# Rational filter and convolution: filter taps by butterflies, and a shifted input copied inside SBUF

## The chip, the cores and the metric

The kernel runs on one core of one Trainium2 chip. The metric is the device time of one execution in microseconds. Three runs of the kernel before took 27,779.66, 27,808.01 and 27,824.27 us; the median is 27,808.01.

## The reference

The input `x` is (4, 512, 512, 16), float32. Layer 0 convolves it over the two image axes with a filter whose transform is a quotient of two short polynomials, then layer 1 applies a 3x3 normalised convolution. Both add their result to their input. Cut to what matters here:

```python
def _L0_conv_ref(x, h0, numerators, denumerator):
    a = jnp.pad(denumerator, ((0, 0), (0, 0), (1, 0), (1, 0)), constant_values=1.0)
    b = jnp.pad(numerators, ((0, 0), (0, 0), (0, 0), (1, 0), (1, 0)), constant_values=0.0)
    H_truncated = jnp.fft.rfft2(b, s=(l1, l2)) / jnp.fft.rfft2(a, s=(l1, l2))
    h_truncated = jnp.fft.irfft2(H_truncated, s=(l1, l2))
    H = jnp.fft.rfft2(h_truncated, s=(2 * l1, 2 * l2))
    H_full = h0 + H[0]
    X = jnp.fft.rfft2(x, s=(2 * l1, 2 * l2), axes=(-3, -2))
    Y = jnp.einsum('...hwi,ijhw->...hwj', X, H_full)
    y = jnp.fft.irfft2(Y, s=(2 * l1, 2 * l2), axes=(-3, -2))
    return y[..., :l1, :l2, :]

x = x + _L0_conv_ref(_gn(x), L0_conv_h0, L0_conv_numerators, L0_conv_denumerator)
x = x + _L1_conv_ref(_gn(x), L1_conv_kernel, L1_conv_bias, L1_conv_radius)
```

`_gn` is a group norm over 8 groups of channels. There are 16 input channels i and 16 output channels j, so 256 filters.

## The kernel before, in words

The Fourier transforms are matmuls with constant matrices, all in float32. A float32 matmul shows as two instructions in the trace. The kernel has five stages, one after the other.

**The filter phase** (`filter_phase`, lines 223 to 430) makes the filter's spectrum `g_d` in DRAM. It loops over the output channel j, over two halves h of the even frequencies of the second axis, and over the input channel i: 16 x 2 x 16 = 512 spectra. For each, `spectrum` evaluates both polynomials by matmuls over 18 rows (`pab`, line 320), copies them out of PSUM on ScalarE (`ab`), and divides: VectorE makes the reciprocal and the products `m` and `sp`, GpSimd makes `dn`, `x` and the sums in `m` (lines 330 to 344). `taps` multiplies `sp` by the constant `dinv` (`pg`, line 353) and ScalarE copies the result into a staging tile `st`. Before the change, `dinv` takes the spectrum over the first axis's frequency k1 straight to the form that the product stage wants: even frequencies of blocks of 8 taps. The calls are staggered by one: `spectrum` of the next i is issued ahead of `taps` of the one before. After all i of a (j, h), `st` is stored to `g_d` (line 405). `odd` loads four blocks of `g_d`, makes the odd frequencies of the second axis (`pt`, line 381, 16 matmuls of 128x512) and stores them. One `odd` call follows every second spectrum, beginning with the second j. The group norm's statistics of `x` are gathered beside the first spectra.

**The forward phase** transforms `x` over the second axis into `x_d`. **The product phase** (`conv_phase`, lines 578 to 763) takes 513 rows of frequencies one at a time, as a pipeline written out in `step(n)`. A row's filter tile is `g`, its input tile `x`. `x_part` transforms four batches of the input over blocks (`px`, line 643) into `xf`. On its last batch GpSimd stores `xf` to a DRAM buffer `xf_d` (line 648). `load_xe` (line 658), issued by SyncE (SP) one step ahead, reads it back as `xe`: eight copies, each shifted by one block of 16 partitions. `g_part` transforms the filter (`pg`, line 675), using the upper and lower 64 partitions as two matmuls of 64x128 with the constant `dg`, into `gh`. `mix` multiplies the two (`pm`, line 691, 32 columns of the array each). `over_q` and `over_g` are the inverse over blocks (`pz`, line 708, and `py`, line 724), and GpSimd stores the result to `y_d`. `evict` copies PSUM to SBUF on VectorE and ScalarE in turn (lines 608 and 610).

**The inverse phase** transforms back over the second axis and **the layer 1 phase** does the rest.

The tile framework places the waits and orders each engine's instructions ahead of time with a scheduler of its own, roughly by the order in the program[...]. SP issues the loads, GpSimd (POOL) the stores of `xf` and of the product.

Of the kernel before, what the change touches and what calls it, by code (L numbers as in the profile page):

```python
# [29 lines left out]
F32 = mybir.dt.float32  # L36
# [15 lines left out]
XF = F * 2 * B  # L52
# [8 lines left out]
def constants():  # L61
# [3 lines left out]

    r = np.array([[v for u in range(8) for v in ((8 * q + u, -(8 * q + u) % S) if q + u else (0, 32))]
                  for q in range(4)])
    k1 = (64 * np.arange(8)[None, :, None] + r[:, None, :]).reshape(-1)
    p9 = np.arange(9)
    ang = 2 * np.pi * np.outer(p9, k1) / N  # L70
    c["e1"] = np.concatenate([np.cos(ang), -np.sin(ang)], 0)
    e2 = np.zeros((4, 32, 2, 2, P))
    a2 = (2 * np.pi * np.outer(p9, np.arange(256)) / N).reshape(9, 2, P)
# [4 lines left out]
    t = np.arange(N)  # L78
    back = np.exp(2j * np.pi * np.outer(k1, t) / N) / N
    over_s = np.exp(-2j * np.pi * np.outer(np.arange(S) - 31.5, 2 * np.arange(33)) / F)  # L80
    d = np.zeros((4, P, 2, 4, 4, 8, 8))
    for cc in range(2):
        taps = (back * (1, 1j)[cc]).reshape(N, S, 8)
        for plane in range(2):
            v = np.einsum("kse,sr->kre", (taps.real, taps.imag)[plane], over_s)
            re, im = v.real[:, :32], np.concatenate([v.imag[:, 32:], v.imag[:, 1:32]], 1)
            for part, w_ in (((0, re), (2, im)), ((3, re), (1, im)))[plane]:
                d[:, :, cc, part] = w_.reshape(4, P, 4, 8, 8)
    c["dinv"] = np.stack([d[q, :, :, :, q] for q in range(4)], 1).reshape(P, -1)

    f_all = 2 * np.pi * np.outer(np.arange(S) - 31.5, np.arange(F)) / F
    dg = np.zeros((4, 32, F))
    for r in range(33):
        full = np.zeros((2, S), complex)
        full[0, r] += 1.0
        full[0, -r % S] += -1.0 if r else 0.0
        full[1, r] += 1j
        full[1, -r % S] += 1j if r < 32 else 0.0
        for part in range(2):
            if r == 32 * (1 - part):  # L100
                continue
            sig = (np.exp(2j * np.pi * np.outer(np.arange(S) - 31.5, 2 * np.arange(S)) / F) @ full[part]) / S
            assert abs(sig.imag).max() < 1e-12
            if part == 0:
                dg[0, r] = dg[3, r] = sig.real @ np.cos(f_all)
            else:
                v = -(sig.real @ np.sin(f_all))
                dg[2, r % 32], dg[1, r % 32] = v, -v
    c["dg"] = dg.reshape(P, F)
# [33 lines left out]
    for q in range(4):  # L143
        for cg in range(2):
            for s0 in range(4):
                co, si = turn(np.array(cg + q * (s0 - 31.5)), 4)
                for j in range(C):
                    q1[q, cg, j, s0, 0, j], q1[q, cg, j, s0, 1, j] = co, si
# [4 lines left out]
    for s0 in range(4):  # L153
        for cx in range(2):
            for c2 in range(2):
                n = gg[:, None] * (s0 - 31.5) + 4 * gg[:, None] * s1[None, :] + 32 * (cx + c2)
                co, si = turn(n, F)
                for b2 in range(2):
                    ig[:, cx, b2, s0, c2, 0, b2, :] = co / F
                    ig[:, cx, b2, s0, c2, 1, b2, :] = si / F  # L160
# [59 lines left out]
def filter_phase(tc, cst, h0, num, den, g_d, beside):  # L220
    nc = tc.nc
    with ExitStack() as ctx:
# [4 lines left out]
        hp = ctx.enter_context(tc.tile_pool(name="f_h", bufs=2))  # L227
        stp = ctx.enter_context(tc.tile_pool(name="f_stage", bufs=3))
# [9 lines left out]
        dinv = load_const(nc, cp, cst, "dinv").rearrange("p (k c n) -> p k c n", k=4, c=2)  # L238
# [108 lines left out]
        def taps(sp, st, i):  # L347

            for kp in range(2):
                pg = ps_g.tile([P, 2, 2, 2 * 64], F32, name="pg")  # L350
                for k in range(2):
                    for c in range(2):
                        nc.tensor.matmul(  # L353
                            pg[:, k].rearrange("p a x -> p (a x)"), sp[:, 2 * kp + k, c, :],
                            dinv[:, 2 * kp + k, c, :], start=(c == 0), stop=(c == 1),
                        )
                for a in range(2):
                    nc.scalar.copy(
                        st[a][:, :, i].rearrange("p (q k x) -> p k q x", q=2, k=4)[:, 2 * kp : 2 * kp + 2],
                        pg[:, :, a].rearrange("p k (q x) -> p k q x", q=2),  # L360
                    )

        def odd(j, tb):

            first = ((0, 96), (64, 32))[tb // 8]
            at = [((first[c] + 4 * (tb % 8)) * C + j) * 8 * C for c in range(2)]
            step = [C * 8 * C, 4], [1, 8 * C]
            ev = evp.tile([P, 2, 2, 32 * C], F32, name="ev_in")
            for h in range(2):
                for c in range(2):  # L370
                    nc.sync.dma_start(
                        out=ev[:, h, c].rearrange("p (s e) -> p s e", s=4),
                        in_=dram(g_d[h], None, at[c], *step),
                    )
            for hh in range(2):
# [13 lines left out]
                for c in range(2):  # L389
                    nc.sync.dma_start(  # L390
                        out=dram(g_d[2 + hh], None, at[c], *step),
# [6 lines left out]
        def finish(j, h, i, sp):  # L398
            nonlocal st
            if i == 0:  # L400
                st = [stp.tile([P, N, C], F32, name=f"st{a}", tag="st") for a in range(2)]
            taps(sp, st, i)
            if i == C - 1:
                for a in range(2):
                    nc.sync.dma_start(
                        out=dram(g_d[h], None, a * G_ROW // 2 + j * 8 * C,
                                 [C * 8 * C, 64], [1, 8 * C]),
                        in_=st[a].rearrange("p (r e) i -> p r (e i)", e=8),
# [634 lines left out]
```

## Time and profile before

| | |
|---|---|
| median of three runs | 27,808.01 us |
| profiled execution, its own time | 27,779.66 us |
| profiled execution, span of the core | 27,777.9 us |
| granted TensorE clock, mean | 0.905 |
| busy: TensorE (PE), VectorE (DVE), ScalarE (ACT), GpSimd (POOL) | 92%, 42%, 28%, 24% |
| steady filter, per spectrum (2000 to 8000 us) | 17.05 us |
| product phase, per step | 21.34 us |

Busy shares are averages over stages that have different limits, so each stage is read on its own. The 40 digits of a slice row are tenths of busy time in slices of 694 us: the filter covers about the first 13, the forward phase up to the 16th, the product phase the 16 after that. A group line gives busy time, mean duration of one instruction, and the idle time of the engine before it with what ended it. "PEld" is the load of weights into TensorE, which runs beside matmuls. In a line of the order in time the first number is the start in us, the second the length, and a bracket names an idle time and its releaser.

### The profile page before, as it was taken

To read this page: it belongs to the slowest core of one execution; us is meant where nothing else is said; L and a number is where in the kernel's file an instruction comes from. 1 tells how busy PE (TensorE), PEld (TensorE's weight loads), DVE (VectorE), ACT (ScalarE), POOL (GpSimd) and SP (SyncE) were. 2 spreads that over 40 slices of the span, in tenths; PEclk is the share of its full clock that TensorE was granted. 3 is DMA by queue.
4 is the path that set the end of the run, shared out by engine and by line. 5 is a ranking of instruction groups with operands and counts; after the bars stand their busy time and mean duration, and the time that the engine had idled before them with its cause. 6 is when DMAs were issued, how large, how long until landed. Compare 5 with 4: busy or idle time off the path is not lost. (4 is left out here: it accounts for less than half of the span.)

```text
span 27777.9 us, 539638 instructions
## 1 busy us (share of the span) xinstructions
PE 25559.6 (92%) x240412; PEld 16342.2 (59%) x240412; DVE 11700.4 (42%) x16077; ACT 7865.0 (28%) x13480; POOL 6775.9 (24%) x8210
## 2 busy tenths in 40 slices
PE   9999999999999999999999999999999999566666
PEld 6556666666665445666666666666666544455556
DVE  6555444544443112333333333333333200577777
ACT  4333333333332111222222222222222100122222
POOL 5444444444442000000000000000000000355555
PEclk8888888888888999999999999999999999766666
DMA  3433333333334334888888888888888633211110
GB/s 97 137 93 98 87 97 88 98 86 100 85 98 129 102 107 150 323 319 321 321 319 323 318 321 318 321 322 320 321 323 322 236 111 111 79 53 54 49 43 21
DMA packets 2987106, 5014.77 MB, mean 181 GB/s; under 512 B 97482, under 2 KB 2064932, under 8 KB 2885958
## 3 DMA queue, kind: packets, MB, share of 16 engines
q1 hardware_dynamic: 2725894, 4105.78, 43.0%
q0 software_dynamic: 203584, 740.22, 6.8%
q10 hardware_dynamic: 55296, 134.24, 1.7%
q8 instruction: 1883, 30.85, 0.4%
q14 instruction: 449, 3.68, 0.0%
HBM read 3502.38 MB, written 1477.44 MB: 179 GB/s over the span
## 5 line engine op out<-in xcount | busy, mean ns | idle before, releaser
L381 PE MATMUL pt<-ev_in,c_todd 128*128 128x512 f32 x8192 | 3683.0, 608 | 52.0 <-DMA ev_in<-g_d 33.8
L353 PE MATMUL pg<-c_dinv,sp 128*128 128x256 f32 x8192 | 2665.3, 492 | 102.5 <-DVE sp L344 91.9
L381 PEld LDWEIGHTS pt<-ev_in,c_todd 128*128 128x128 f32 x8192 | 1589.2, 195 | 1977.5 <-issue 1879.5
L675 PEld LDWEIGHTS pg<-c_dg,g 64*128 64x128 f32 x32832 | 2040.3, 189 | 1061.2 <-issue 965.2
L675 PE MATMUL pg<-c_dg,g 64*128 64x128 f32 x32832 | 2461.8, 287 | 139.2 <-issue 138.5
L353 PEld LDWEIGHTS pg<-c_dinv,sp 128*128 128x128 f32 x8192 | 2012.2, 253 | 855.0 <-issue 327.9
L691 PEld LDWEIGHTS pm<-xe,gh 128*32 128x32 f32 x131328 | 1899.9, 110 | 1043.8 <-issue 1037.5
L708 PE MATMUL pz<-c_iq,yf 128*128 128x128 f32 x16416 | 2419.8, 291 | 73.2 <-issue 63.6
L945 PE MATMUL pc<-l_band,xn 128*128 128x160 f32 (+3 forms) x9024 | 1824.3, 370 | 714.4 <-DVE e_y L968 713.5
L333 DVE RECIPROCAL dn<-dn 128x256 f32<-128x256 f32 x1024 | 1786.7, 1745 | 1637.8 <-POOL dn L332 1637.7
L648 POOL DMA_DIRECT2D xf_d<-xf x513 | 365.9, 713 | 8524.6 <-ACT xf L610 4284.9
L608 DVE COPY gh<-pg 128x512 f32<-128x512 f32 x2052 | 1419.5, 692 | 2060.7 <-PE pg L675 2060.7
L320 PE MATMUL pab<-c_e,u 18*128 18x256 f32 x8192 | 2223.3, 428 | 54.0 <-ACT ab L325 53.9
L724 PE MATMUL py<-z,c_ig 128*64 128x256 f32 x8208 | 2242.4, 705 | 2.1 <-ACT z L610 1.4
L691 PE MATMUL pm<-xe,gh 128*32 128x64 f32 x131328 | 2084.7, 220 | 168.8 <-issue 164.6
L708 PEld LDWEIGHTS pz<-c_iq,yf 128*128 128x128 f32 x16416 | 2016.6, 193 | 331.5 <-issue 77.6
L643 PE MATMUL px<-c_dfs,x 128*128 128x512 f32 x4104 | 2136.1, 602 | 29.2 <-issue 16.5
L945 PEld LDWEIGHTS pc<-l_band,xn 128*128 128x128 f32 x9024 | 1556.0, 240 | 973.5 <-DVE e_y L968 740.0
L320 PEld LDWEIGHTS pab<-c_e,u 18*128 18x128 f32 x8192 | 1641.3, 207 | 631.5 <-issue 262.4
L610 ACT COPY gh<-pg 128x512 f32<-128x512 f32 x2052 | 1201.2, 585 | 2189.3 <-PE pg L675 2189.3
L556 PE MATMUL pf<-xw,c_fwd 128*128 128x512 f32 x4096 | 1781.5, 593 | 3.7 <-DVE xw L547 3.7
L792 PE MATMUL po<-c_inv,yt 128*128 128x512 f32 x4096 | 1760.3, 593 | 14.2 <-DMA yt<-y_d 14.2
(149 smaller groups left out, 27208.7 us busy)
## 6 DMA issues: line engine op xcount, KB each, us to landing
xe<-xf_d SPq DMA_DIRECT2D x513, 4096.0 KB, 14.2
xf_d<-xf POOLq DMA_DIRECT2D x513, 1024.0 KB, 6.4
g<-g_d SPq DMA_DIRECT2D x511, 1024.0 KB, 5.5
g_d<-st SPq DMA_DIRECT2D x64, 4096.0 KB, 31.4
ev_in<-g_d SPq DMA_DIRECT2D x1024, 256.0 KB, 4.8
g_d<-ot SPq DMA_DIRECT2D x1024, 256.0 KB, 2.3
xt<-in_x SPq DMA_DIRECT2D x128, 1024.0 KB, 9.7
x_d<-xo SPq DMA_DIRECT2D x128, 1024.0 KB, 5.1
```

The source lines that it names most:

```text
L320: nc.tensor.matmul(pp[:, k].rearrange("p c n -> p (c n)"), us[n][q, k1 : k1 + P], e2[q, h, :], start=True, stop=True,)
L333: nc.vector.reciprocal(dn, dn)
L353: nc.tensor.matmul(pg[:, k].rearrange("p a x -> p (a x)"), sp[:, 2 * kp + k, c, :], dinv[:, 2 * kp + k, c, :], start=(c == 0), stop=(c == 1),)
L381: nc.tensor.matmul(pt, todd[:, kc, m : m + P], ev[:, kc % 2, kc // 2], start=(kc == 0), stop=(kc == 3),)
L556: nc.tensor.matmul(pf.rearrange("p i s t -> p (i s t)"), fwd[:, w, col : col + P], xw[:, w, 4 * i4 : 4 * i4 + 4, :].rearrange("p i h -> p ...
L643: nc.tensor.matmul(px.rearrange("p l f c -> p (l f c)"), t[:, b], dfs.rearrange("p l n -> p (l n)"), start=True, stop=True)
L675: nc.tensor.matmul(pg[c][:, k], g[half, 4 * j4 + k], dg[half], start=True, stop=True)
L691: nc.tensor.matmul(pm[32 * q : 32 * q + 32, gi], gh[:, f].rearrange("p c j -> p (c j)"), xe[:, :, f, :], start=True, stop=True,)
L708: nc.tensor.matmul(pz[:, t], y[:, at].rearrange("p g x -> p (g x)"), iq, start=True, stop=True)
L724: nc.tensor.matmul(py[64 * half : 64 * half + 64, odd], ig[:, s0, c2], z[:, :, :, 2 * s0 + c2, :].rearrange("p t h j -> p h j t"), start=( ...
L792: nc.tensor.matmul(po, yt[kc][:, m // 4, odd, bh, :], inv[:, kc, :], start=(kc == 0), stop=(kc == 7),)
L945: nc.tensor.matmul(pc[:, lo:hi, :].rearrange("p w j -> p (w j)"), blocks[q][0][:, h * P + dh : h * P + dh + P], bands[dh][:, o : o + hi - ...
```

## The change

The filter's `dinv` no longer includes the transform over blocks. `taps` first combines the four quarters of k1 (a radix-4 butterfly: `s` and `w` of the even outputs on GpSimd, `d` and `w` of the odd ones on VectorE), then multiplies each of the four results by a 128-point transform; `st` holds taps in their natural order. `g_part` then does the whole transform of a block with the constant `dfs` that `x_part` uses, over all 128 partitions, in eight calls of two matmuls in place of four calls of eight; `dg` is gone. `x_part` stores nothing: `load_xe` copies `xf` to `xe` inside SBUF by 15 transfers issued on SP. `over_g` reads `z` with the 16 output channels innermost in place of the 8 block positions, and its eviction puts them in the old order. The `pg` pool of the product phase has two banks in place of three, the `pz` pool two in place of one. The constants `iq` and `ig` lose a shift of 31.5 blocks.

```diff
         def taps(sp, st, i):
-            for kp in range(2):
-                pg = ps_g.tile([P, 2, 2, 2 * 64], F32, name="pg")
-                for k in range(2):
+            s = bt.tile([P, 2, 2, P], F32, name="s")
+            d = bt.tile([P, 2, 2, P], F32, name="d")
...
+            nc.gpsimd.tensor_add(fl(s), fl(sp[:, 0:2]), fl(sp[:, 2:4]))
+            nc.vector.tensor_sub(fl(d), fl(sp[:, 0:2]), fl(sp[:, 2:4]))
+            w = hp.tile([P, 4, 2, P], F32, name="w")
+            nc.gpsimd.tensor_add(w[:, 0], s[:, 0], s[:, 1])
+            nc.gpsimd.tensor_sub(w[:, 2], s[:, 0], s[:, 1])
+            nc.vector.tensor_sub(w[:, 1, 0], d[:, 0, 0], d[:, 1, 1])
+            nc.vector.tensor_add(w[:, 1, 1], d[:, 0, 1], d[:, 1, 0])
+            nc.vector.tensor_add(w[:, 3, 0], d[:, 0, 0], d[:, 1, 1])
+            nc.vector.tensor_sub(w[:, 3, 1], d[:, 0, 1], d[:, 1, 0])
+            for rp in range(2):
+                pg = ps_g.tile([P, 2, 2, P], F32, name="pg")
+                for r2 in range(2):
+                    r = 2 * rp + r2
                     for c in range(2):
                         nc.tensor.matmul(
-                            pg[:, k].rearrange("p a x -> p (a x)"), sp[:, 2 * kp + k, c, :],
-                            dinv[:, 2 * kp + k, c, :], start=(c == 0), stop=(c == 1),
+                            pg[:, r2].rearrange("p c t -> p (c t)"), w[:, r, c, :],
+                            dinv[:, r, (1 - c) * P : (3 - c) * P],
+                            start=(c == 0), stop=(c == 1),
                         )
-                for a in range(2):
+                for c in range(2):
                     nc.scalar.copy(
-                        st[a][:, :, i].rearrange("p (q k x) -> p k q x", q=2, k=4)[:, 2 * kp : 2 * kp + 2],
-                        pg[:, :, a].rearrange("p k (q x) -> p k q x", q=2),
+                        st[c][:, :, i].rearrange("p (t r) -> p r t", r=4)[:, 2 * rp : 2 * rp + 2, :],
+                        pg[:, :, c, :],
                     )
...
-        ps_g = ctx.enter_context(tc.tile_pool(name="h_psg", bufs=3, space=PSUM))
+        ps_g = ctx.enter_context(tc.tile_pool(name="h_psg", bufs=2, space=PSUM))
...
-        ps_z = ctx.enter_context(tc.tile_pool(name="h_psz", bufs=1, space=PSUM))
+        ps_z = ctx.enter_context(tc.tile_pool(name="h_psz", bufs=2, space=PSUM))
...
             if b == B - 1:
-                dst = xf_d[n % 4]
-                nc.gpsimd.dma_start(
-                    out=bass.AP(tensor=dst.tensor, offset=dst.offset,
-                                ap=[[XF, P], [P * XF, 2], [1, XF]]),
-                    in_=state.pop(("xf", n)).rearrange("p l f h c k -> p l (f h c k)"),
-                )
                 del state["x", n]
         def load_xe(n):
             xe = xep.tile([P, 8, F, 2 * B], F32, name="xe")
-            src = xf_d[n % 4]
-            nc.sync.dma_start(
-                out=xe.rearrange("p t f x -> p t (f x)"),
-                in_=bass.AP(tensor=src.tensor, offset=src.offset,
-                            ap=[[XF, P], [C * XF, 8], [1, XF]]),
-            )
+            xf = state.pop(("xf", n)).rearrange("p l f h c k -> p l (f h c k)")
+            for k in range(8):
+                m = P - C * k
+                nc.sync.dma_start(out=xe[:m, k].rearrange("p f x -> p (f x)"), in_=xf[C * k :, 0])
+                if k:
+                    nc.sync.dma_start(out=xe[m:, k].rearrange("p f x -> p (f x)"), in_=xf[: C * k, 1])
...
-            pg = [ps_g.tile([P, 4, F], F32, name=f"pg{c}", tag="pg") for c in range(2)]
-            for k in range(4):
-                for c in range(2):
-                    half = slice(64 * c, 64 * c + 64)
-                    nc.tensor.matmul(pg[c][:, k], g[half, 4 * j4 + k], dg[half], start=True, stop=True)
-            for c in range(2):
-                evict(gh[:, :, c, 4 * j4 : 4 * j4 + 4], pg[c].rearrange("p j f -> p f j"))
+            pg = ps_g.tile([P, 2, F * 2], F32, name="pg")
+            for k in range(2):
+                nc.tensor.matmul(pg[:, k], g[:, 2 * j2 + k], dfs[:, 0], start=True, stop=True)
+            evict(gh.rearrange("p f c j -> p j (f c)")[:, 2 * j2 : 2 * j2 + 2], pg)
...
-            py = ps_y.tile([P, 2, 2, C, 8], F32, name="py")
+            py = ps_y.tile([P, 2, 2, 8, C], F32, name="py")
...
-                            z[:, :, :, 2 * s0 + c2, :].rearrange("p t h j -> p h j t"),
+                            z[:, :, :, 2 * s0 + c2, :].rearrange("p t h j -> p h t j"),
...
-            evict(yo, py.rearrange("p o h j t -> p (o h j t)"))
+            evict(yo.rearrange("p (x j t) -> p x j t", x=4, j=C), py.rearrange("p o h t j -> p (o h) j t"))
...
                 if after:
-                    g_part(n + 1, k)
+                    g_part(n + 1, 2 * k)
                 if soon:
                     over_q(n - 1, k)
                 if late:
                     x_part(n + 2, k)
+                if after:
+                    g_part(n + 1, 2 * k + 1)
```

## The prediction

> **What bounds the kernel now.** I read the page first (busy shares, slices, groups by cost), then busy time by stage, then the order in time inside the two stages that the change touches: the filter phase (0 to 8720 us, where the last `g_d<-st` store is issued) and the spectral product `conv_phase` (about 10,950 to 21,900 us).
>
> ```profile
> span 27777.9 us, 539638 instructions
> PE   9999999999999999999999999999999999566666
> DVE  6555444544443112333333333333333200577777
> PEclk8888888888888999999999999999999999766666
> ```
>
> TensorE is busy nine tenths or more of both stages, but in the first 13 slices, the filter, its clock is only 0.8. Why shows in 3 us windows of the filter (columns: length, then busy PE, PEld, DVE, ACT, POOL, then granted clock, DMA share, GB/s):
>
> ```profile
> 5074.00:5077.00 3.00, 3.00 (x8) 2.07 (x7) 3.00 (x4) 0.83 (x2) 2.06 (x4) 0.50 0.00 0
> 5086.00:5089.00 3.00, 3.00 (x9) 1.33 (x8) 0.00 (x0) 0.58 (x1) 0.00 (x0) 1.00 0.17 50
> ```
>
> There are two kinds of stretch. In one VectorE never rests and TensorE does `pab` and `pg` at half clock; in the other TensorE runs the odd-frequency matmuls `pt` at full clock while VectorE and GpSimd rest. The order in time gives the cycle:
>
> ```profile
> 5048.69 12.18 PE L381 MATMUL pt<-ev_in,c_todd 128*128 128x512 f32 x28
> 5060.80 3.72 PE L320 MATMUL pab<-c_e,u 18*128 18x256 f32 x16
> 5064.44 5.41 PE L353 MATMUL pg<-c_dinv,sp 128*128 128x256 f32 x16
> 5069.78 4.78 PE L320 MATMUL pab<-c_e,u 18*128 18x256 f32 x16
> ```
> ```profile
> 5072.53 0.93 DVE L342 TENSOR_TENSOR sp<-m,dn 128x256 f32<-128x256 f32 x1 [0.62 <-POOL m L340]
> 5073.49 0.58 DVE L344 COPY sp<-z 128x8 f32<-128x8 f32 x1
> ```
>
> Two spectra and one odd block take about 34 us (window 2000 to 8000: 22 pairs of stores, so 352 spectra, 17.05 us each). The second spectrum's `sp` is done at 5074.07 and its `pg` starts at 5074.49: **no margin** between the elementwise chain and TensorE there. The chain of the spectrum after it runs under the `pt` burst.
>
> In `conv_phase` a step of 21.34 us repeats 513 times, and TensorE's work fills it:
>
> ```profile
> 15011.20 4.29 PE L724 MATMUL py<-z,c_ig 128*64 128x256 f32 x16
> 15015.42 2.00 PE L691 MATMUL pm<-xe,gh 128*32 128x64 f32 x128
> 15017.35 1.16 PE L675 MATMUL pg<-c_dg,g 64*128 64x128 f32 x16
> 15018.44 1.16 PE L708 MATMUL pz<-c_iq,yf 128*128 128x128 f32 x8
> 15019.44 1.02 PE L643 MATMUL px<-c_dfs,x 128*128 128x512 f32 x2
> ```
>
> From start to start: 4.22, 1.93 (twice a step), 1.09, 1.00 and 0.95 (four times each), 20.2 us in all. The DMA engines are 85% busy. `xe` is issued 15017.96 and takes 14.2 us, so lands at 15032.2; the next step's `mix` starts at 15036.77: 4.6 us of slack.
>
> ```profile
> xe<-xf_d SPq DMA_DIRECT2D x373, 4096.0 KB, 14.2
> q1 hardware_dynamic: 496141, 2057.01, 69.0%
> ```
>
> [...] `sp` takes 349 ns at least and 985 at most, the longest when it starts beside a GpSimd operation of some 720.
>
> ```profile
> L342 DVE TENSOR_TENSOR sp<-m,dn x2048: 349/426/985, 41.5 to 8703.3; 128x256 f32<-128x256 f32 x187
> L339 POOL TENSOR_TENSOR m<-m x1024: 712/724/1108, 36.1 to 8701.5; 128x256 f32<-128x256 f32 x171
> ```
>
> [...] `py` reads its moving side at a step of 1 KB and takes 705 ns; other matmuls of 256 columns take 380 in the median (`pg`, line 353).[...] 16 of the half-height `pg` start over 1.09 us, 68 ns each, though one takes 272; 16 `py` over 4.22 us, 264 each, though one takes 705.[...]
>
> **The change, part by part.** Sums are made against the profiled execution (27,779.66 us, span 27,777.9), the fastest of the three runs; the median lies 28 us above, which I add at the end.
>
> *Filter, matmuls.* `taps` keeps 8 matmuls of 128x256 and 4 ScalarE copies of 256 elements per spectrum; the copies write at a step of 256 B in place of 64 B. ScalarE is 37% busy here (741 of 2000 us): nothing. The loads and stores of `odd` move the same bytes in the same runs: nothing.
>
> *Filter, butterflies.* Added per spectrum, on GpSimd: one sum of 128x512 (nearest row line 917, 1.32 us; I take 1.35) and two of 128x256 (0.71 each): 2.8 us. On VectorE: one difference of 128x512 (0.62, the least of line 336) and four of 128x128 (0.22 each, extrapolated from 349 ns for 256 elements and 616 for 512): 1.5 us. All have two SBUF inputs[...]: 4.3 us.[...] ten GpSimd operations of 0.71 and, on VectorE, 2 x 0.62 + 4 x 0.35: 9.8 us. In j=0, with no odd block between (stores at 216.4 and 394.8 us), a spectrum takes 11.15 us[...].
>  - j=0: 32 spectra, each 4.3/0.88 = 4.9 us longer: **+155 us**.
>  - The other 240 pairs: the first spectrum's butterflies fall under the `pt` burst, where VectorE and GpSimd rest some 12 us; the second's lie between `sp` and `pg`, where there is no margin. `pg` waits 4.3 us more, and the `pt` behind it on TensorE waits too, unless the tile scheduler, which already moves single `pt` matmuls ahead of a late `pg` (x4 at 5041.90), fills the gap. Bounds per pair: 0 (all filled) to 10 (both spectra exposed). I take 3.0, most of one wait: 240 x 3.0 = **+720 us**.
>
> *conv_phase, g.* Eight half-height matmuls of 128 columns per quarter step, which overlap in pairs, become four full-height ones of 256 columns. Price: the same shape at full clock in the filter, 3.65 us for 16 instructions, 0.228 each; 8 x 0.228 = 1.82 in place of 1.09 us. Four quarters: +2.94 us a step. Eight evictions a step stay eight (0.69 and 0.59 us each, VectorE 34% and ScalarE 29% busy): hidden.
>
> *conv_phase, py.* Runs of 16 floats. `mix` already reads runs of 8 floats with no visible loss: 128 instructions of 64 columns in 1.93 us, 60 ns per four. So I price `py` as overlapping pairs at 0.228: 8 x 0.228 = 1.82 in place of 4.22: -2.4 us. Bounds: -0.6 (no overlap, 16 x 0.228 = 3.65) to -2.6.
> Net +0.54 us a step; x 513 = **+277 us**. The second `pz` bank and the third `pg` bank given up: waits on both sum to under 15 us of TensorE time: nothing.
>
> *conv_phase, xe.* GpSimd's store of `xf` (0.71 us to issue) and one SP issue of 0.37 us become 15 SP issues, 5.6 us at that price. They wait only for the last `xf` eviction (about 15012), so the last is out near 15018, when the single one is issued today, and ahead of the next `g` load (15029.6). The queues move 5.8 MB a step in place of 6.8. A 4 KB packet costs 178 ns (69.0% of 16 engines over 8000 us / 496,141). If every engine is kept fed, 1024 rows take 64 x 178 = 11.4 us. If pieces go strictly one after another[...]: 18.5 us. The other loads and stores (1.57 MB at 321 GB/s) take 4.9 us. So 16.3 to 23.4 us against a step of 21.9: I take the middle, hidden by TensorE.
>
> **Sum:** 27,780 + 155 + 720 + 277 = 28,932; plus 28: **28,960 us**.
>
> **Rivals.**
>  - *Butterflies queue behind the next spectrum* on VectorE and GpSimd[...]; then both chains of a pair are exposed: 240 x 9.8 = 2350 + 155 + 277: 30,590. For: VectorE has no gap in the `pab`/`pg` stretch. Against: 12 us of rest per pair are free.
>  - *The copies bind:* 23.4 us a step, +1.5 over TensorE's 21.9: +770, giving 29,730. For: DMA at 85% now.[...]
>  - *Runs of 16 change nothing* (the change doesn't do what it says): `py` stays, +2.94 x 513 = 1510, with 875 of the filter: 30,190. Against: `mix`.
>  - *Faster:* the lighter DMA load ends TensorE's "issue" gaps (383 us over the phase, 0.75 us a step), `py` gains 2.6, so a step is 0.4 us shorter (-205), and `pt` matmuls fill every wait, with j=0 at +60: 27,660. It decides once the filter costs less than the product phase gains: 205 us, which leaves 145 or 0.6 us per pair beside j=0.
>
> **How the numbers follow.** Forecast 0.50 (own range 28,500 to 29,500); queued butterflies 0.15; copies 0.15; runs without effect 0.08; the faster mechanism 0.12, of which half ends beyond 0.2% (56 us, about what a measurement of this kernel can tell from no change) and most of the rest inside it. So faster 0.06, same 0.05, slower 0.89. Range 27,950 (filter +155 alone, product unchanged) to 30,600.
>
> **What would show it.** After: `pg` (line 353's successor) with 1 us or more of idle per spectrum behind `w`;[...] `py` near 380 ns a matmul and under 2 us a step; `pg` of 128x256 at 7.3 us a step; `mix` not waiting for `xe`. Wrong if the step grows past 22.5 us with `mix` waiting on DMA, or if the filter ends before 9000 us.

## The result, and the profile after

| | before | after |
|---|---|---|
| median of four runs | 27,810.23 us | 31,492.83 us |
| range of the runs | 27,779.66 to 27,824.27 us | 31,411.45 to 31,562.68 us |
| span of the profiled execution | 27,777.9 us | 31,409.7 us |
| last `g_d<-st` store issued (filter's end) | 8,717.2 us | 9,929.2 us |
| first to last `py` (product phase) | 10,953.2 us, 21.39 per step | 13,399.7 us, 26.17 per step |

The changed kernel is slower: the ratio is 1.1325, 95% interval 1.1296 to 1.1354. Of the 3,632 us between the two spans the filter takes 1,212 and the product phase 2,446; the rest is 26 us shorter. The forecast had 875 and 277 there. So the direction was right, the filter's term too small by 337 us, and the product phase wrong by 2,169.

The head of the page of the changed kernel (span, then tenths of busy time, now in slices of 785 us):

```profile
span 31409.7 us, 519548 instructions
PE   7899999999999999888888888888888889866666
DVE  7665555555554112333333333333333320177778
PEclk7888888888888999999999999999999999976666
DMA  2433232323233335888888888888888863311110
```

In the product phase (slices 17 to 33) TensorE falls from 9 to 8, and yet the DMA engines are no busier than before and VectorE has two thirds of its time free. From 14,000 to 21,000 us TensorE is idle for 4.0 us of a step (0.8 before), and its own work takes 22.2 us (20.6 before) at a mean granted clock of 0.92 (0.99 before). So most of the time went into waiting. The groups by cost say where (busy time, mean of one in ns, idle time ahead of it and what ended it; `mix` writes `pm`). First three groups of the kernel before, then those of the changed kernel:

```profile
L691 PE MATMUL pm<-xe,gh 128*32 128x64 f32 x131328 | 2084.7, 220 | 168.8 <-issue 164.6
L353 PE MATMUL pg<-c_dinv,sp 128*128 128x256 f32 x8192 | 2665.3, 492 | 102.5 <-DVE sp L344 91.9
L608 DVE COPY gh<-pg 128x512 f32<-128x512 f32 x2052 | 1419.5, 692 | 2060.7 <-PE pg L675 2060.7
```
```profile
L658 PE MATMUL pm<-xe,gh 128*32 128x64 f32 x131328 | 2548.6, 238 | 1962.1 <-issue 1960.7
L643 PE MATMUL pg<-c_dfs,g 128*128 128x256 f32 x16416 | 4121.7, 390 | 24.3 <-issue 23.5
L335 PE MATMUL pg<-c_dinv,w 128*128 128x256 f32 x8192 | 3016.0, 530 | 640.6 <-POOL w L323 384.4
L587 DVE COPY gh<-pg 128x512 f32<-128x512 f32 x2052 | 2107.2, 1027 | 2744.8 <-PE pg L643 2744.8
```

The line of `pg<-c_dinv,w` has the filter's wait that the prediction named. The line of `pm` has what is new: 1,961 us of idle time ahead of `mix` that ended in "issue", no semaphore; before, it was 164.6 us. TensorE was not waiting for `xe`. The operations by tile show the issues of the copies (min, median, max in ns, then first and last start) and who waited for them (us, times):

```profile
L631 SPq DMA_DIRECT2D xe<-xf x4104: 496/588/3002, 12130.3 to 25545.2; - x196
L633 SPq DMA_DIRECT2D xe<-xf x3591: 493/662/4864, 12131.4 to 25545.8; - x200
  PEld pm L658: 55.4, 144
```

The order in time from the end of one step into the next (start, length, operation, then idle time ahead):

```profile
18019.54 1.95 PE L691 MATMUL py<-z,c_ig 128*64 128x256 f32 x16
18021.41 2.00 PE L658 MATMUL pm<-xe,gh 128*32 128x64 f32 x128
18023.34 1.13 PE L619 MATMUL px<-c_dfs,x 128*128 128x512 f32 x2
18024.40 1.76 PE L658 MATMUL pm<-xe,gh 128*32 128x64 f32 x107
18030.76 0.53 PE L658 MATMUL pm<-xe,gh 128*32 128x64 f32 x21 [4.60 <-issue]
18031.22 1.77 PE L619 MATMUL px<-c_dfs,x 128*128 128x512 f32 x2
18032.79 1.91 PE L643 MATMUL pg<-c_dfs,g 128*128 128x256 f32 x4
```

Two things are to be seen. `py` takes 1.9 us as forecast. And **the four `mix` calls of a step now stand nearly in a row** (128 records are two calls), with one `px` between. Before, two calls stood at the head of a step (the `pm` at 15015.42 in the prediction) and two in its middle:

```profile
15022.48 1.02 PE L643 MATMUL px<-c_dfs,x 128*128 128x512 f32 x2
15023.43 1.99 PE L691 MATMUL pm<-xe,gh 128*32 128x64 f32 x128
15025.35 1.16 PE L675 MATMUL pg<-c_dg,g 64*128 64x128 f32 x16
```

In the midst of the stream of the changed kernel TensorE stops for 4.60 us, and the `px` after it takes 1.77 in place of 1.13.

**What the pauses are.** The change does not touch the order by hand, but the tile scheduler sets it anew. The page of the changed kernel lists a queue for instructions among the DMA queues:

```profile
PE 26943.2 (86%) x223996; PEld 18117.7 (58%) x223996; DVE 13909.7 (44%) x18637; ACT 8714.5 (28%) x13480; POOL 8074.4 (26%) x9231
q8 instruction: 1762, 28.87, 0.4%
```

q8 has 1,762 packets, each of 16 KB. TensorE's matmuls and weight loads are 447,992, and with its semaphore records, which the page does not count, 451,133: 256.0 records to a packet. In the kernel before, 1,883 packets stand against 482,160 records, 256.1 to each. I read from this that q8 carries TensorE's own instructions, in blocks of 256. Number TensorE's records from the first (matmuls, weight loads and semaphores) and count them in blocks of 256. Between 13,000 and 21,000 us the changed kernel pauses 325 times for over 1.5 us, always at one and the same place of the block (the 193rd or 194th). In 320 of these pauses a packet of q8 lands inside, in the other five at most 0.15 us ahead. In the median the transfer starts 1.0 us after TensorE stopped and takes 1.26 us, and TensorE goes on 1.44 us after it has landed; the pause is 3.7 us. These pauses sum to 1,166 us, 3.8 per step. Over the whole phase all but 1 us of the 1,961 ahead of `mix` stand at this place. The kernel before has 58 such pauses, 120 us: they were there to be seen. What makes the transfer start so late was not separated.

The DMA view of the window 18026 to 18031, which holds the pause, has the packet; that of 18020 to 18026 has none:

```profile
q1 hardware_dynamic: 339, 1.10, 85.8%
q0 software_dynamic: 80, 0.26, 15.7%
q8 instruction: 1, 0.02, 1.4%
```

Most of the rest of the lost time is the half clock after a pause. The longer the pause, the more often it came: 1 us after the pause the granted clock is one half behind 133 of the 135 pauses of 4 us or more, behind 59 of the 74 of 3 to 4 us, behind 31 of the 69 of 2 to 3, and behind 7 of the 47 that were shorter. Behind the pause of 4.60 us `px` takes 1.77 us, behind one of 2.43 us in the step before it still takes 1.13. In all, the clock is at one half for 1,236 of the 8,000 us, against 96 in the kernel before.

### The profile page after: what moved, and what is told of

It reads as the page before. It is cut to its first block, busy times and chain, and to the rows that moved or that the text cites. A ratio compares the mean times of both kernels' runs of the same rounds, so it can differ in the third digit from the quotient of the medians.

```text
span 31409.7 us, 519548 instructions
## 1 busy us (share of the span) xinstructions
PE 26943.2 (86%) x223996; PEld 18117.7 (58%) x223996; DVE 13909.7 (44%) x18637; ACT 8714.5 (28%) x13480; POOL 8074.4 (26%) x9231
## 3 DMA queue, kind: packets, MB, share of 16 engines
q8 instruction: 1762, 28.87, 0.4%
## 4 chain that ended last, share of the span: by engine, by line
PE 61%; DVE 14%; POOL 11%; issue 10%; DMA 3%; ACT 1%; SPq 0%; DVEq 0%; ACTq 0%; POOLq 0%
PE pg L643 11%; PE pm L658 7%; PE pt L363 7%; PE px L619 7%; PE pf L538 6%; PE po L761 6%; PE pz L675 5%; PE py L691 3%; PE pg L335 3%; DVE dn L298 3%; DVE e_r L947 2%; PE pab L285 2%; DVE sp L307 2%; POOL dn L297 1%; PE pn L921 1%
## 5 line engine op out<-in xcount | busy, mean ns | idle before, releaser
L658 PE MATMUL pm<-xe,gh 128*32 128x64 f32 x131328 | 2548.6, 238 | 1962.1 <-issue 1960.7
L643 PE MATMUL pg<-c_dfs,g 128*128 128x256 f32 x16416 | 4121.7, 390 | 24.3 <-issue 23.5
L643 PEld LDWEIGHTS pg<-c_dfs,g 128*128 128x128 f32 x16416 | 3135.6, 199 | 993.1 <-issue 671.5
L335 PE MATMUL pg<-c_dinv,w 128*128 128x256 f32 x8192 | 3016.0, 530 | 640.6 <-POOL w L323 384.4
L587 DVE COPY gh<-pg 128x512 f32<-128x512 f32 x2052 | 2107.2, 1027 | 2744.8 <-PE pg L643 2744.8
L335 PEld LDWEIGHTS pg<-c_dinv,w 128*128 128x128 f32 x8192 | 2072.8, 267 | 1770.7 <-POOL w L323 584.2
L589 ACT COPY gh<-pg 128x512 f32<-128x512 f32 x2052 | 2109.0, 1028 | 2847.6 <-PE pg L643 2847.6
L619 PE MATMUL px<-c_dfs,x 128*128 128x512 f32 x4104 | 2641.9, 729 | 67.9 <-issue 58.8
L587 DVE COPY yf<-pm 128x512 f32<-128x512 f32 x1026 | 707.0, 689 | 3223.0 <-PE pm L658 3216.8
L341 ACT COPY st<-pg 128x256 f32<-128x256 f32 x2048 | 1068.5, 629 | 3075.3 <-PE pg L335 3053.0
## 6 DMA issues: line engine op xcount, KB each, us to landing
xe<-xf SPq DMA_DIRECT2D x1026, 256.0 KB, 9.2
ev_in<-g_d SPq DMA_DIRECT2D x1024, 256.0 KB, 4.8
```

The source lines that it names most:

```text
L335: nc.tensor.matmul(pg[:, r2].rearrange("p c t -> p (c t)"), w[:, r, c, :], dinv[:, r, (1 - c) * P : (3 - c) * P], start=(c == 0), stop=(c ...
L587: nc.vector.tensor_copy(dst, src)
L589: nc.scalar.copy(dst, src)
L619: nc.tensor.matmul(px.rearrange("p l f c -> p (l f c)"), t[:, b], dfs.rearrange("p l n -> p (l n)"), start=True, stop=True)
L643: nc.tensor.matmul(pg[:, k], g[:, 2 * j2 + k], dfs[:, 0], start=True, stop=True)
L658: nc.tensor.matmul(pm[32 * q : 32 * q + 32, gi], gh[:, f].rearrange("p c j -> p (c j)"), xe[:, :, f, :], start=True, stop=True,)
```

## The experiments

Theories for the product phase: **O**, the order (four `mix` calls together) costs the time, by whatever mechanism; **T**, the copies' traffic does, in any order; later, once the pauses were read, **F**, TensorE's instructions arrive late. For the filter: **W**, the wait of `pg` for `w`; **P**, the added work in the queues of VectorE and GpSimd. Step lengths are first to last `py` over 512. "Pauses at the fetch" are those of over 1.5 us at the 193rd or 194th record, counted from 13,000 to 21,000 us in every run.

**Order without copies, copies without the rest.** Three kernels: the changed kernel with the store to and load from DRAM put back; the same with the `mix` calls together; the kernel before with nothing but the copies.

```
-  for k in range(8):                       # changed kernel -> DRAM
-      nc.sync.dma_start(out=xe[:m, k]..., in_=xf[C * k :, 0])
...
+  nc.gpsimd.dma_start(out=bass.AP(tensor=dst.tensor, ...), in_=state.pop(("xf", n))...)
+  nc.sync.dma_start(out=xe..., in_=bass.AP(tensor=src.tensor, ...))
...
-  if here and k % 2 == 0:                  # together
-      mix(n, k)
-      mix(n, k + 1)
+  if here and k == 0:
+      for q in range(4):
+          mix(n, q)
```

> The kernel after with the input going through DRAM as before (one store by GpSimd, one load of 4 MB), all else as after; the scheduler then puts two mix calls, other work, two mix calls. Both O and T expect the step near TensorE's work of 20.2 us plus 0.8 of issue gaps, 21 us, and a total of 28,700 to 29,000 us: what is left above the kernel before is then the filter's 1.2 ms. If the step stays above 23 us, the copies are not the cause at all and g_part or its eviction (1.03 us in place of 0.69 and 0.59) is.

> As a_dram, but with the four mix calls of a step together in the program, and so in a row on TensorE. Theory O: the issue gaps ahead of pm come back, 3 to 4 us a step, the total is above 30,300 us. Theory T: no gaps beyond those of a_dram, total within 1% of a_dram.

> The kernel before with the 15 SBUF copies alone in place of the store to DRAM and the load (filter, g_part and over_g as before). The scheduler again puts the four mix calls in a row. O and T: issue gaps of 3 to 5 us a step and half-clock work after them, step 24.5 to 26.5 us, total 29,500 to 30,500 us, so most of the product phase's loss is the copies' doing. Forecast of the prediction (copies hidden): 27,700 to 27,900 us.

Measured: 29,728.61 us (1.0702, 1.0684 to 1.0720), 31,555.69 (1.1366, 1.1347 to 1.1385) and 31,013.73 (1.1168, 1.1152 to 1.1185). Steps: 22.72, 26.39 and 27.78 us. So the order alone, without one copy, brings back the whole loss (+3.67 us a step); and the copies alone, put into the kernel before, bring the order with them and the loss too. The first run and the last lay above what I had expected. In the first, `mix` waits 684 us over the phase for the load of `xe` from DRAM, which the expectation had left out; in the last, `py` also waits for the evictions of `z`, and what else lengthens its step was not separated. The group of `mix` in the first, then the head of a step in the last:

```profile
L667 PE MATMUL pm<-xe,gh 128*32 128x64 f32 x131328 | 2231.7, 229 | 791.4 <-DMA xe<-xf_d 683.9 <-issue 101.8 <-DVE yo L590 3.1
```
```profile
18003.59 2.00 PE L685 MATMUL pm<-xe,gh 128*32 128x64 f32 x128
18005.52 1.12 PE L643 MATMUL px<-c_dfs,x 128*128 128x512 f32 x2
18006.58 0.97 PE L685 MATMUL pm<-xe,gh 128*32 128x64 f32 x50
18012.14 2.35 PE L685 MATMUL pm<-xe,gh 128*32 128x64 f32 x78 [4.59 <-issue]
```

Lines of a step of the "together" kernel, in order of time:

```profile
18003.69 3.62 PE L667 MATMUL pm<-xe,gh 128*32 128x64 f32 x228
18011.32 0.64 PE L667 MATMUL pm<-xe,gh 128*32 128x64 f32 x28 [4.01 <-issue]
18011.89 1.86 PE L652 MATMUL pg<-c_dfs,g 128*128 128x256 f32 x4
18013.55 1.92 PE L684 MATMUL pz<-c_iq,yf 128*128 128x128 f32 x8
18026.70 1.03 PE L652 MATMUL pg<-c_dfs,g 128*128 128x256 f32 x4
```

The pause costs 4.01 us, and the `pg` and `pz` behind it take 1.86 and 1.92 where later in the step they take 1.03 and 1.05: another 1.7. Its packets of q8 take 0.94 us, 0.3 less than beside the copies, and start 2.1 us into the pause. It is not the copies that make the packet late.

**Copies with the old order.** The changed kernel, with its order forced to two and two calls. Beside it the kernel before with the new reading of `py` alone.

```
+  for k in (0, 2):
+      mix(n, k)
+      mix(n, k + 1)
+      with tc.issue_after(state["last_m"]):
+          rest(k)          # g, q and x parts of the quarter
+          rest(k + 1)
...
-  py = ps_y.tile([P, 2, 2, C, 8], F32, name="py")     # kernel before
+  py = ps_y.tile([P, 2, 2, 8, C], F32, name="py")
```

> The kernel after with its 15 copies, and the rest of each step tied behind the mix calls that precede it in the program, so that TensorE's order is exactly that of a_dram: two mix calls, half the other work, two mix calls, the other half. Theory O (four mix calls in a row outrun the loading of TensorE's instructions): the issue gap ahead of pm falls from 1961 us to under 300; what is left is the copies' own time, 22.4 us of DMA a step, which then shows as a wait of mix on xe; step 22.5 to 23.5 us, total 29,600 to 30,200 us. Theory T (copies hold up instruction loads in any order): gaps stay over 1500 us and the total over 31,000.

> The kernel before with over_g alone changed: runs of 16 in py's moving side, and the eviction that puts them back. py goes from 4.2 to 1.9 us a step as in the profile after; the load of xe, 20.2 us from the last xf eviction to landing, allows a step of 18.4 us. Expected step 18.9 to 19.5 us, total 26,500 to 26,900 us, faster than both kernels. If DMA (18.1 us busy a step) binds first, 27,000 to 27,300.

Measured: 31,109.80 us (1.1200, 1.1184 to 1.1217) and 27,644.02 (0.9951, 0.9936 to 0.9966). O misses here, and so does my estimate for `py`. With two and two calls the pauses at the fetch are halved (from 325 to 156, from 1,166 to 583 us), but waits on `g`, `xe` and `x` take their place, and the total lies where T had it: O alone was not the answer while the copies are there. And `py`, 2.3 us shorter, gives 0.23 us a step: what it frees turns into waits, as the group of `mix` in that kernel shows. Of its pauses, 156 (401 us) stand at the fetch, where the kernel before has 58.

```profile
L691 PE MATMUL pm<-xe,gh 128*32 128x64 f32 x131328 | 2176.7, 225 | 741.4 <-DMA xe<-xf_d 458.7 <-issue 281.9
```

**The calls one by one.** If F holds, the same instructions spread evenly need no pause. Two kernels, with copies and with DRAM, each with one `mix` call ahead of each quarter of the other work.

```
+  for k in range(4):
+      with tc.issue_after(state["last_g"]):
+          mix(n, k)
+      with tc.issue_after(state["last_m"]):     # with the copies only
+          rest(k)
```

> The changed kernel with its 15 copies; the four mix calls of a step stand one by one, each ahead of its own quarter of the other work, and that order of TensorE's instructions is forced. Nothing is left out. Theory F (TensorE's instructions are late): in the changed kernel each of the 442 pauses of over 1.5 us between 13,000 and 24,000 us stands at the same one of each 256 instruction records, a 16 KB packet of the instruction queue lands in the pause, and TensorE goes on some 1.4 us later; four mix calls in a row are 512 records in 4 us[...]. Spread out, the pauses go; what is left is 20.2 us of TensorE's work and 22.4 us of DMA time per step, so a step of 22.5 to 23 us in place of 26.3: 29,500 to 29,900 us in all. Theory T (the traffic of the copies holds TensorE's work up, whatever the order): the pauses turn into waits on transfers, as in the run with two and two calls: about 31,100 us.

> The changed kernel with the old way through DRAM in place of the copies, and the mix calls one by one in forced order. Nothing is left out. It has 18.1 us of DMA time and 20.2 us of TensorE's work per step. Theory F: the pauses at the fetch go (76 of them, 276 us, in the run with two and two calls), and the order takes no more: a step of 20.5 to 21.5 us, 29,000 to 29,600 us in all, up to 700 us below the two-and-two version (29,729). Theory T says nothing of it but that it is not above 29,729. If it comes out at 29,700 or more, the wait on the load of xe through DRAM (684 us) is what sets the step, and the fetch is of no account once the calls stand two and two.

Measured: 30,608.89 us (1.1017, 1.1001 to 1.1034) and 29,454.66 (1.0602, 1.0586 to 1.0618); steps of 24.54 and 22.31 us. With the copies the pauses at the fetch fall from 325 to 53 (1,166 to 128 us), with DRAM from the 304 of the together order (1,353 us) to 19 (41 us). F stands. But the first run came out 700 us above the expected range: 153 other pauses ahead of `mix` are left, most of them waits on `g`, `x` and `xe`, and a second limit shows. In the table by stage (length, busy PE, PEld, DVE, ACT, POOL, granted clock, DMA share, GB/s), 14,000 to 21,000 us:

```profile
14000.00:21000.00 7000.00, 6217.61 (x98038) 4701.56 (x98038) 2455.55 (x2992) 2280.98 (x2993) 153.75 (x285) 0.95 0.95 237
```

The DMA engines are 95% busy, 23.3 us of a step. All transfers together bring only 237 GB/s, where the kernel before has 321 at a share of 0.85. The packets of 4 KB in q1, which in this kernel are those of the copies, take 270 ns each in the mean; in the kernel before, those of the load of `xe` from DRAM take 173.

**Half the bytes.** To tell the copies' DMA time from their number, each of the 15 carries half; the calls stay one by one.

```
-  xe = xep.tile([P, 8, F, 2 * B], F32, name="xe")
+  xe = xep.tile([P, 8, F // 2, 2 * B], F32, name="xe")
-  nc.sync.dma_start(out=xe[:m, k]..., in_=xf[C * k :, 0])
+  nc.sync.dma_start(out=xe[:m, k]..., in_=xf[C * k :, 0, : F * B])
```

> The version of the changed kernel with its copies and with the mix calls one by one; each copy brings only the first half of its frequencies (2 KB in place of 4 KB of a partition), and the mix reads those twice, so half of the result is another. There are 15 copies a step still. Theory of the DMA engines (with the pauses at the fetch gone, the 24.5 us of a step are the copies' time on the DMA engines, 95% busy): about 10 us of DMA time go, TensorE's 20.2 us bind, a step of 20.5 to 21.5 us, 28,500 to 29,100 us in all. Rival, the number of the copies (SP's queue, in which the 15 issues stand ahead of the loads of x and g): the step stays at 24 us or above, 30,300 us or more.

Measured: 28,773.19 us (1.0355, 1.0339 to 1.0370), a step of 21.01 us, as the theory of the DMA engines had it; 24 pauses at the fetch are left (47 us). In the same table TensorE is now 99% busy at full clock, with a DMA share of 0.61:

```profile
14000.00:21000.00 7000.00, 6916.30 (x114357) 5223.22 (x114347) 2867.76 (x3491) 2667.15 (x3492) 180.50 (x333) 1.00 0.61 177
```

**The filter.** Two kernels test W: `pg` reads `sp` and not `w`, so that nobody waits for the butterflies; and the butterflies traced straight behind their own spectrum. Two leave out one engine's half of them.

```
-  pg[:, r2]..., w[:, r, c, :],
+  pg[:, r2]..., sp[:, r, c, :],                        # nobody waits
+  pg[:, r2]..., (w if r % 2 else sp)[:, r, c, :],      # GpSimd's half out
+  pg[:, r2]..., (sp if r % 2 else w)[:, r, c, :],      # VectorE's half out
-  sp = spectrum(us, z, h, i)
+  sp = fly(spectrum(us, z, h, i))                      # straight behind
```

> The kernel after, but pg of the filter reads sp in place of w: the butterflies are still computed, in full, and nothing waits for them; the filter it computes is another one. Theory W (TensorE's wait for the last butterfly is the cost): the filter's 1212 us fall below 450, total under 30,800 us. Theory P[...]: 800 us or more of it stays, total above 31,050 us.

> The kernel after, with the butterflies traced straight behind their own spectrum, ahead of the next one's elementwise work on VectorE and GpSimd; same instructions. Theory W: pg's idle behind w (641 us over the phase) falls below 250 and the total by 300 us or more, to 31,200 or less. Theory P: total within 150 us of the kernel after.

> The changed kernel with POOL's half of the butterflies left out: s and the even rows of w are not computed, and the matmuls of those rows read sp in their place, so the filter is another. VectorE's half stays. The filter's end is read (9929 us changed, 8717 us before). Theory P1 (what is added to POOL's queue, 3.2 us per spectrum, delays dn and with it the next spectrum): most of the 1212 us goes, the filter ends at 8,700 to 9,100 us and the whole at 30,300 to 30,700 us. Theory P2 (what is added to VectorE's queue, about 3.1 us per spectrum, delays the reciprocal and the evictions): little goes, 9,600 to 9,900 us, the whole at 31,200 to 31,500. Both halves alike[...]: about 9,300.

> The changed kernel with VectorE's half of the butterflies left out: d and the odd rows of w are not computed, and the matmuls of those rows read sp in their place, so the filter is another. POOL's half stays. The filter's end is read: 9929 us changed, 8717 before, 9248 with POOL's half left out, so POOL's half stands for 681 of the 1212 us. Theory P1 (POOL's queue alone, VectorE's half is dear only because POOL's runs beside it): VectorE's half gives less than the missing 531 us, the filter ends at 9,500 to 9,800. Theory of the sum (each half costs its own length in the chain): 9,400 us, as 9929 less 531. Theory of the longer half (the wait for w ends with whichever comes last): far less than 531, about 9,800 to 9,900.

| | median us | ratio, interval | filter's end us |
|---|---|---|---|
| nobody waits | 31,718.86 | 1.1415, 1.1395 to 1.1434 | 9,965.6 |
| straight behind | 31,433.59 | 1.1318, 1.1301 to 1.1335 | 9,700.9 |
| GpSimd's half out | 30,988.37 | 1.1153, 1.1137 to 1.1170 | 9,247.8 |
| VectorE's half out | 31,074.27 | 1.1181, 1.1164 to 1.1197 | 9,347.0 |

W falls. When `pg` waits for nothing, the filter is no shorter; the wait only moves to the `pt` behind it, which now waits for its evictions `ot` on VectorE, where the butterflies stand too (first the changed kernel, then this one):

```profile
L363 PE MATMUL pt<-ev_in,c_todd 128*128 128x512 f32 x8192 | 3896.9, 629 | 87.2 <-DVE ot L368 45.0
L363 PE MATMUL pt<-ev_in,c_todd 128*128 128x512 f32 x8192 | 4002.6, 646 | 863.6 <-DVE ot L368 825.1
```

The halves give 681 and 582 us, 1,263 together against the 1,212 that the change costs: the theory of the sum, each half pays its own length in the chain. An earlier place gives back 228, though the wait of `pg` for `w` stays (668 us, 641 in the changed kernel). The totals gain less than the filters, or lose more, since the product phase of these four kernels, whose code there is that of the changed kernel, takes 26.6 to 26.8 us a step against its 26.17. Its pauses at the fetch sum to 1,247 to 1,270 us against 1,166; why was not traced. So a difference of up to 0.6 us a step between kernels with the calls in a row can't be put down to what was changed in them.

Why VectorE's share is so long shows in its butterflies in the changed kernel, and without GpSimd's beside them (the same line stands four lines higher there):

```profile
L325 DVE TENSOR_TENSOR w<-d 128x128 f32<-128x128 f32 x512 | 400.7, 783 | 15.5 <-DVE d L321 0.5
L327 DVE TENSOR_TENSOR w<-d 128x128 f32<-128x128 f32 x512 | 317.2, 619 | 0.0
```
```profile
L321 DVE TENSOR_TENSOR w<-d 128x128 f32<-128x128 f32 x512 | 194.7, 380 | 13.8
L323 DVE TENSOR_TENSOR w<-d 128x128 f32<-128x128 f32 x512 | 209.6, 409 | 0.0
```

The same operation takes 783 ns in the mean beside GpSimd's butterflies, and 380 without them. In the kernel before, `sp` shows the same on a smaller scale: the 1,641 of its operations that overlapped one of GpSimd took 639 ns in the mean, the 407 that overlapped none 419.

**A version that beats both.** The kernel before, the new reading of `py`, and the `mix` calls one by one; then with the four `x_part` of a step in its first half, so that the store of `xf` goes out earlier.

```
-  x_part(n + 2, k)
+  if late and k < 2:
+      x_part(n + 2, 2 * k)
+      x_part(n + 2, 2 * k + 1)
```

> The kernel before with the new order of reading in the last inverse step alone, and the mix calls one by one. Nothing is left out. The reading alone gave 27,644 us: TensorE's work is 19.0 us per step, yet it idles behind the load of xe (459 us) and behind nothing visible (some 960 us in pauses over 1.5 us between 13,000 and 24,000 us). Theory F: of these, 480 us stand at the fetch and go: 27,000 to 27,400 us. A rival, the DMA engines: at 18.1 us of DMA time per step they are nearly as full as TensorE, and the pauses only turn into longer waits on xe: 27,600 us, no change.

> The kernel before with the new order of reading in the last inverse step, the mix calls one by one, and the four x parts of a step in its first half, so that the store of xf goes out some 9 us earlier. Nothing is left out. In the version without the early x parts (27,415 us, 20.66 us per step) TensorE waits 532 us in 8,000 for the load of xe, since store (8.1 us) and load (14.1 us) follow on each other and take more than a step. Theory C (this chain): the wait goes, a step of 19.2 to 19.8 us, 26,700 to 27,000 us. Rival D (the DMA engines, 84% busy): the load only takes longer, 27,300 us or more.

Measured: 27,414.99 us (0.9869, 0.9853 to 0.9886) and 27,333.86 (**0.9836**, 0.9820 to 0.9852), steps of 20.66 and 20.57 us. Spreading the calls is worth 0.8% beyond `py`, and ends just above the range of F. The early store took most of the wait on `xe` away, from 422 to 105 us between 14,000 and 20,000, as C had it, but little time with it: the time lies where D had it. TensorE is 95% busy and the DMA engines 88%; what holds the step at 20.57 us was not separated further.

## Why the prediction was wrong

Taken together, by step of the product phase: `py` alone -0.23 (to 21.16), then `g` and the rest of the change with the DRAM path +1.56 (22.72), the order +3.67 (26.39), the copies in that order -0.22 (26.17), which is less than kernels with one and the same product phase differ by. In the other orders the copies cost more: 2.9 us a step with two and two calls (25.60 against 22.72), 2.2 one by one (24.54 against 22.31).

 - **Filter, j=0**: 155 us forecast, from 4.3 us of added work over 0.88, the share that 9.8 us of work have of a spectrum's 11.15. That the work of VectorE and GpSimd simply adds up was my estimate; no run shows it. The second store of `g_d` is issued at 509.7 us in place of 394.8: 115.
 - **Filter, the pairs**: 3.0 us each forecast; 1,212 - 115 over 240 pairs is 4.6. That the butterflies lengthen a chain that has no margin was right, and 4.6 lies inside the bounds of 0 to 10; the size was too small. TensorE's idle time per pair grew by 2.2 us (7,000 us less its busy time, over 179 pairs against 205), under the 3.0 of the one exposed wait. The same matmuls take 2.8 us more of busy time (36.5 against 33.7 per pair), at a granted clock of 0.82 in place of 0.87; both are of 1,500 to 8,500 us, where a pair costs 5.0 more. The sum had no term for a slower clock behind a wait. "`pg` idle behind `w` by 1 us or more" came true, yet was not the cause: with that wait taken away the filter is no shorter.
 - **`g`**: priced at 1.82 us a quarter, measured 1.73 start to start. The evictions were taken at 0.69 and 0.59 us and take 1.03 each, as the lines of `gh` above show for VectorE; `pg` waits 24 us in all, so they stay hidden from it.
 - **`py`**: 1.82 forecast, 1.88 measured, a mean of 386 ns each where it was 705 in the order of reading before. Its worth was wrong: 0.23 us a step and not 2.4, since the sum held TensorE to be short of nothing else.
 - **`xe`, the step that failed**: "I take the middle, hidden by TensorE". The sum put the copies at nothing; with them the step takes 26.17 us, without them 22.72. The landing was in time, as said (`mix` waits 55 us in all), and the DMA time of a step, 22.2 us, was inside the bounds of 16.3 to 23.4, though the upper one rested on 18.5 us for pieces one after another, an estimate of mine that no run shows, and the price of a packet, the mean of all of q1, came from loads out of DRAM: 178 ns, where the copies' packets take 257 in the changed kernel. But the working moved 15 DMA issues and asked only when they land. It did not ask what the scheduler does with TensorE's order when `xe` comes later, nor whether TensorE's instructions come as fast as it runs them. The 164.6 us of "issue" ahead of `mix` were in the profile of before, and were named in the faster rival as a thing the DMA load causes; they were TensorE's fetch, as 162 of them stand at its place in the block. Why the scheduler's plan puts the calls together was not traced; that the copies alone suffice for it, the kernel before with only the copies shows.
 - **SP's queue**: 0.37 us an issue forecast, 0.59 and 0.66 measured in the median.
 - **The rivals**: "the copies bind at 23.4 us" had the second limit nearly right. It lay hidden under the pauses, and shows at 24.5 us once most of them are gone. Even so that kernel takes 30,609 us, just past the top of the range. Of the signs of a wrong forecast, the long step came, but with `mix` waiting for nothing that has a name.

## What to carry to other kernels

Look for idle time that ends in "issue" in the midst of a stream of small matmuls: here it was 1,961 us ahead of `mix`, a loss of its own. Count the instruction records there, not only the microseconds (the four calls of a step are 512 of TensorE's), and try the dense runs apart, with longer matmuls between them: here that took the pauses from 325 to 53. When a transfer is replaced, compare the order of every engine before and after, since the scheduler may set work together that was apart; and after one limit is removed, look for the next one that it covered, as the DMA engines here, 95% busy once the pauses were gone. A wait that a trace names need not be the cost: take it away before you price it. Without the wait of `pg` for `w`, 641 us, the filter ended at 9,965.6 us, and with it at 9,929.2.

## What the runs showed of the hardware

 - 256 of TensorE's records ran in some 2 us in `mix`. With four calls in a row TensorE paused at the fetch about once a step (325 and 304 times in 8,000 us), for 3.7 us in the median at a DMA share of 0.85 (the changed kernel) and for 4.4 at 0.73 (the together order without copies). A pause of 4.0 us in the latter cost about 1.7 more in half-clock matmuls.
 - Packets of 4 KB from SBUF to SBUF took 270 ns each in the kernel with copies and calls one by one, against 173 from DRAM in the kernel before. Part of that may be the fuller DMA engines (95% against 85%): the 8 KB packets of the other loads went from 367 to 469 ns. The two were not separated.
 - VectorE's and ScalarE's eviction of 128x512 took 1,027 and 1,028 ns when it wrote single values 64 B apart, and 692 and 585 before, in runs of four; the order in which they read PSUM differs too. The eviction of `yf`, which did not change, took 689 on VectorE, and 692 before.
